# Weight sums of two outer products moved from GpSimd to VectorE, with a shorter lookahead around them

## The chip, the cores and the metric

The kernel runs on one core of one Trainium2 chip. The core has a matrix engine (TensorE, PE in the profile; its weight loads are a row of their own, PEld), VectorE (DVE), ScalarE (ACT), GpSimd (POOL) and SyncE (SP), which here issues most DMAs. Each engine works through its own queue in order, and semaphores order the engines among each other. The metric is the device time of a launch in microseconds.

## The reference

Two residual layers over x of shape (2, 2048, 512), all in fp32. Biases and selections are cut to what matters:

```python
def layer0(x):                       # wi, wo chosen by type_label (one of 3 used), swi, swo shared
    s0 = relu(x @ swi[0]) @ swo[0]   # 512 -> 2048 -> 512
    s1 = relu(x @ swi[1]) @ swo[1]
    eo = relu(x @ wi[label]) @ wo[label]
    gate_in = concat([eo[:, 0], s0[:, 0], s1[:, 0]])
    w = softmax(relu(gate_in @ g1) @ g2)
    return eo * w[0] + s0 * w[1] + s1 * w[2]

x = x + layer0(x)
x = x + (x @ W[cat] + b[cat])        # 512 -> 512, one matrix for each batch entry
```

Nearly all the work is in the three two-matrix layers of `layer0`.

## The kernel before

**Units.** The tokens are cut into four blocks of 1024. A unit is one block through one pair of matrices. There are twelve: shared pair 0 over four blocks (units 0 to 3), shared pair 1 over four, and the pairs chosen by the label over two blocks each. A unit has a first half `up` (x times the first matrix, then ReLU; "kind 0" in the code) and a second half `down` (times the second matrix; "kind 1").

**Products.** Each multiplication is a two-level block scheme that needs 7 products instead of 8 at each level: 7 outer products `i`, each with 7 inner products `k`, so 49 weight tiles (128 x 4 x 128) for each half. Products 1, 2 and 4 of a level use plain blocks of the weights; products 5, 6, 7 and 3 use sums and differences of blocks. `make_tops` (L726) and `outer_sum` (L912) make the sums on the side of the activations on VectorE; they are 128x1024 sums in `down`.

**The first unit.** Units 1 to 3 load ready sums of the weights from the scratch tensors `ws`. Unit 0 has none and makes them on the chip (class `First`, L507). `outer2` and `sum_of` make an outer sum of a whole quarter of the matrix, as four sums of 128x512 for kind 1, on GpSimd, in place of a quarter that is read no more. `take` (L598) gives one weight tile: for `k` of 1, 2 or 4 a view of the quarter in SBUF; for `k` of 5, 6, 7 or 3 it calls `make` (L621), which makes one 128x512 sum into a new buffer of the pool `w` (12 buffers). `make` also queues a store of the tile to `ws`, on SP; `flush(3)` holds the last three stores back. In `down` of unit 0 the outer products come in the order 1, 2, 3, 7, 6, 5, 4, and each needs four such sums. In the text below (2; 5) is the inner sum 5 of outer product 2.

**Order of the work.** `SLOTS_DN` (L433) is an order written out by hand: 49 slots of four matmuls each. In `down` (L894) a slot issues its matmuls (L945), then calls `used_w` (L642), then issues the eviction of its result from PSUM. The evictions on VectorE are L959 (`dz`, the seed of another accumulation), L967 (`ds`, a snapshot), L969 (`y`, block y22, which the slot of product 3 needs before it can write the same bank), L976 and L978 (`y`). After the eviction comes one step of a job, the activation sums of the next outer product (L744 to L751, L916). `y_sums` (L922) are sums of results near the end of the half.

`used_w` counts the weight tiles used, over both halves, and lets `fetch_w` (L469) go twelve tiles ahead; for unit 0 `fetch_w` calls `take`. So the place of a weight sum in the queue of its engine is set by how far `fetch_w` runs ahead. `may` (L593) holds back the first tile of outer products 3 and 7 until the last tile of products 1 and 2 is used, since their outer sums overwrite those quarters.

In `make` line 630 chooses the engine: in `up` GpSimd for outer products 4 and 3, VectorE for the others; in `down` GpSimd for all.

**Beside it.** In the same half TensorE transposes the next block of x (L309) in eight slots, ScalarE evicts what needs no sum, and at the end GpSimd begins the activation sums of the next unit (`x_sums`, L361).

Of the kernel before, what the change touches and what calls it, by code (L numbers as in the profile page):

```python
# [18 lines left out]
NP = 7  # L19
# [17 lines left out]
def cond_resid_kernel(  # L37
# [22 lines left out]
    nc = tc.nc  # L60
# [395 lines left out]
    def ready(e, kind, part, need):  # L456

        if (e, kind) not in preps:
            return e == 0
        prep = preps[e, kind]  # L460
        if prep.left[part] and need:
            while prep_bg[0] is not prep:
                for other in "ost":
                    prep_bg[0].force(other)
                prep_bg.pop(0)
            prep.force(part)
        return not prep.left[part]

    def fetch_w(upto):  # L469
        while w_next[0] < min(upto, len(w_order)):  # L470
            n, kind, i, k = w_order[w_next[0]]
            e = units[n][0]
            si, sk = SLOT_A[i], SLOT_A[k]
            part = ("t" if sk >= 4 else "s") if si >= 4 else "o" if sk >= 4 else None
            if n == 0 and not begin.may(kind, i, k, w_used[0]):
                return
            if part and not ready(e, kind, part, w_next[0] < w_used[0] + 2):
                return
            w_next[0] += 1
            if n == 0 and begin.take(kind, i, k):  # L480
                continue
            t = wp.tile([P, NG, P], F32, tag="w", name=f"w_{n}_{kind}_{i}_{k}")
            flat = t.rearrange("p g f -> p (g f)")
            if si >= 4 and sk >= 4:
                nc.sync.dma_start(out=flat, in_=ws[e, kind, "t"][:, (si - 4) * 4 + sk - 4, :])
            elif si >= 4:
                nc.sync.dma_start(out=flat, in_=ws[e, kind, "s"][:, (si - 4) * 4 + sk, :])
            elif sk >= 4:
                nc.sync.dma_start(out=flat, in_=ws[e, kind, "o"][:, PLAIN_A[si] * 4 + sk - 4, :])
            else:  # L490
                (a, c), (b, d) = divmod(si, 2), divmod(sk, 2)
                row, col = 2 * a + b, 2 * c + d
                if kind == 0 and e < 2:
                    nc.sync.dma_start(out=flat, in_=swi_v[:, e * DC + row, col, :])
                elif kind == 0:
                    src = wi_v[:, bass.ds(label[e - 2] * DC + row, 1), col, :]
                    nc.sync.dma_start(out=flat, in_=src.rearrange("p o f -> p (o f)"))
                elif e < 2:
                    nc.sync.dma_start(
                        out=t, in_=swo_v[:, e * 4 + row, :, col * P : (col + 1) * P]  # L500
                    )
                else:
                    src = wo_v[:, bass.ds(label[e - 2] * 4 + row, 1), :, col * P : (col + 1) * P]
                    nc.sync.dma_start(out=t, in_=src.rearrange("p o g f -> p (o g) f"))
            w_tiles[n, kind, i, k] = t

    class First:  # L507
# [73 lines left out]
        def outer2(self, i):  # L581
            q = lambda k: self.q[1, k]
            make = lambda *args: self.sum_of(nc.gpsimd, 1, *args)
            if i == 2:
                yield from make(5, self.space2, q(0), q(4), ADD)
                yield from make(6, q(0), q(5), q(1), SUB)
            elif i == 3:
                yield from make(3, q(1), q(2), q(6), SUB)
            elif i == 7:

                yield from make(7, q(2), q(4), q(6), SUB)
# [29 lines left out]
        def make(self, kind, i, k, blk):  # L621
            t = wp.tile([P, NG, P], F32, tag="w", name=f"w_0_{kind}_{i}_{k}")
            self.made[kind, i, k] = t
            x0, x1, op = {
                5: lambda: (blk[0], blk[4], ADD),
                6: lambda: (self.made[kind, i, 5], blk[1], SUB),
                7: lambda: (blk[1], blk[0], SUB),
                3: lambda: (blk[2], self.made[kind, i, 6], SUB),
            }[k]()
            eng = nc.gpsimd if kind == 1 or i in (4, 3) else nc.vector  # L630
            eng.tensor_tensor(t, x0, x1, op)
            self.flush(3 if kind else 1)
            si, sk = SLOT_A[i], SLOT_A[k] - 4
            if si < 4:
                o = ws[0, kind, "o"][:, PLAIN_A[si] * 4 + sk, :]
            else:
                o = ws[0, kind, "t"][:, (si - 4) * 4 + sk, :]
            self.late.append((o, t.rearrange("p g f -> p (g f)")))

    w_used = [0]  # L640

    def used_w():  # L642
        w_used[0] += 1
        fetch_w(w_used[0] + 12)

# [106 lines left out]
    def up(n, xg, tops, y):  # L754
# [12 lines left out]
        for j, i in enumerate(I_UP(n)):  # L767
# [32 lines left out]
            for s, (bk, k, d) in enumerate(SEQ_UP):  # L800
# [17 lines left out]
                if all(kk != k for _, kk, _ in SEQ_UP[s + 1 :]):  # L818
                    used_w()
# [74 lines left out]
    def down(n, H, tops, y, prepare):  # L894
# [39 lines left out]
        def slot(i, name):  # L934
# [9 lines left out]
            for g in range(NG):  # L944
# [6 lines left out]
                    skip_group_check=True,  # L951
                )
            used_w()
            if k == 1:
                z = bank[i, "z"] = ps.tile([P, TQ], F32, tag="z", name=f"dz_{n}_{i}")
# [431 lines left out]
```

## Time and profile before

| | |
|---|---|
| median of three runs | 2229.15 us (2228.36 to 2230.01) |
| the profiled execution | 2225.8 us |
| its span, first to last instruction | 2224.0 us |
| mean granted clock of TensorE | 0.997 |
| first half of unit 0 (to the first matmul of L945) | 0 to 113.55 us |
| second half of unit 0 (to the next unit's first matmul) | 113.55 to 212.10 us |

A line of the page's groups gives the source line, the engine, the operation and the shapes; a line of a timeline gives start, duration, engine, line, operation, output <- input, the count, and in brackets the idle time before it with what ended it. The durations of instructions that wait for a shared resource hold that wait. The granted clock is a share of TensorE's full clock.

### The profile page before, as it was taken

The numbers are of one execution on the slowest core, as the hardware profiler recorded it, in microseconds if no ns is written. First come the engines' busy times: TensorE is split into PE (matmuls) and PEld (weight loads), VectorE is DVE, ScalarE is ACT, GpSimd is POOL, SyncE is SP. The second block draws the span as 40 slices with busy tenths as digits, with TensorE's granted clock in tenths as the row PEclk, the third lists the DMA queues.
The fourth block names the chain that finished last, engine by engine and source line by source line (L and its number), as shares of the span: only waits on it lengthen the run. The fifth ranks groups of instructions, "written<-read, shape, count | busy, mean of one in ns | idle before, by whom it ended". The sixth has DMA issues, their size and how long they took to land.

```text
span 2224.0 us, 29253 instructions
## 1 busy us (share of the span) xinstructions
PE 2184.7 (98%) x9808; PEld 1851.8 (83%) x9808; DVE 1627.8 (73%) x2047; ACT 544.3 (24%) x937; POOL 811.9 (37%) x1259
## 2 busy tenths in 40 slices
PE   8999999999999999999999999999999999999999
PEld 6787888888888888888888888888877877887785
DVE  7897787687587587588587588588676746867695
ACT  3221231331321321231231141131133133213310
POOL 5887533852840540450450451360033023002400
PEclk9999999999999999999999999999999999999999
DMA  9853997997996996896997997896896697679681
GB/s 341 319 178 98 340 326 218 340 328 233 298 306 211 316 315 200 285 328 185 294 316 223 302 302 236 272 337 205 298 297 192 185 314 237 183 236 318 215 282 52
DMA packets 484256, 581.59 MB, mean 262 GB/s; under 512 B 28552, under 2 KB 316296, under 8 KB 480908
## 3 DMA queue, kind: packets, MB, share of 16 engines
q1 hardware_dynamic: 480380, 572.91, 79.4%
q10 hardware_dynamic: 3728, 6.82, 0.9%
q8 instruction: 80, 1.31, 0.2%
q14 instruction: 68, 0.56, 0.1%
HBM read 421.80 MB, written 157.81 MB: 261 GB/s over the span
## 4 chain that ended last, share of the span: by engine, by line
PE 85%; DVE 7%; DMA 2%; issue 1%; SPq 0%; ACT 0%; DVEq 0%; ACTq 0%
PE dx L945 23%; PE ux L810 23%; PE dy L945 11%; PE uy L810 11%; PE dz L945 6%; PE uz L810 6%; PE po L1159 5%; DVE h L916 1%; DMA w<-ws_t 1%; DVE h L787 1%; DVE t L749 1%; DMA w<-in_L_cond_W_dram 1%; DVE t L747 1%; DVE t L744 1%; DVE t L751 0%
## 5 line engine op out<-in xcount | busy, mean ns | idle before, releaser
L810 PE MATMUL ux<-xs,w 128*128 128x256 f32 x1792 | 426.2, 380 | 10.0 <-DVE uz L827 5.0
L945 PE MATMUL dx<-t,w 128*128 128x256 f32 x1680 | 397.4, 379 | 3.3 <-DVE ds L967 3.1
L810 PEld LDWEIGHTS ux<-xs,w 128*128 128x128 f32 x1792 | 338.9, 190 | 69.8 <-DVE uz L827 8.0
L945 PEld LDWEIGHTS dx<-t,w 128*128 128x128 f32 x1680 | 318.1, 190 | 48.7 <-issue 2.4
L1196 POOL TENSOR_TENSOR mix<-mix 128x512 f32<-128x512 f32 x72 | 110.1, 1531 | 443.0 <-ACT mix L1191 355.3
L833 DVE TENSOR_TENSOR us<-ux,h 128x512 f32<-128x512 f32 x240 | 163.2, 687 | 128.3 <-PE ux L810 128.0
L916 DVE TENSOR_TENSOR h<-h,h 128x1024 f32<-128x1024 f32 x192 | 246.4, 1297 | 0.0
L781 ACT ACTIVATE h<-h 128x1024 f32<-128x1024 f32 x156 | 163.9, 1054 | 235.0 <-DVE h L838 122.4
L810 PE MATMUL uy<-xs,w 128*128 128x256 f32 x896 | 212.5, 380 | 2.1 <-DVE h L857 1.9
L838 DVE TENSOR_TENSOR h<-uy,us 128x512 f32<-128x512 f32 x168 | 116.0, 691 | 119.6 <-ACT us L831 115.5
L692 POOL TENSOR_TENSOR seen<-pulse 1x1 f32<-1x1 f32 x33 | 16.9, 513 | 509.7 <-DVE pulse L691 473.2
L810 PEld LDWEIGHTS uy<-xs,w 128*128 128x128 f32 x896 | 169.7, 190 | 30.0 <-DVE h L857 4.3
L844 ACT ACTIVATE h<-uz 128x512 f32<-128x512 f32 x168 | 99.5, 592 | 351.4 <-PE uz L810 312.2
L945 PE MATMUL dy<-h,w 128*128 128x256 f32 x672 | 159.7, 381 | 4.2 <-DVE y L969 4.1
L810 PE MATMUL ux<-xi,w 128*128 128x256 f32 x640 | 152.2, 380 | 5.1 <-DVE us L833 2.9
L945 PEld LDWEIGHTS dy<-h,w 128*128 128x128 f32 x672 | 127.4, 190 | 22.8 <-issue 5.2
L945 PE MATMUL dx<-h,w 128*128 128x256 f32 x616 | 145.5, 379 | 0.0
L945 PE MATMUL dz<-h,w 128*128 128x256 f32 x616 | 145.5, 379 | 0.0
L857 DVE TENSOR_TENSOR h<-uy,us 128x512 f32<-128x512 f32 x168 | 112.1, 686 | 44.0 <-PE uy L810 42.2
L810 PEld LDWEIGHTS ux<-xi,w 128*128 128x128 f32 x640 | 120.5, 190 | 25.1 <-issue 7.2
L141 POOL TENSOR_TENSOR po<-pr 128x384 f32<-128x384 f32 x48 | 54.5, 1136 | 232.5 <-DMA pr<-in_L_cond_wo_dram 82.4
L787 DVE TENSOR_TENSOR h<-h,h 128x1024 f32<-128x1024 f32 x96 | 135.4, 1410 | 3.2 <-ACT h L844 1.9
(155 smaller groups left out, 3432.9 us busy)
## 6 DMA issues: line engine op xcount, KB each, us to landing
w<-ws_t SPq DMA_DIRECT2D x352, 256.0 KB, 4.2
w<-ws_s SPq DMA_DIRECT2D x270, 256.0 KB, 4.2
w<-ws_o SPq DMA_DIRECT2D x264, 256.0 KB, 4.6
xs<-xs SPq DMA_DIRECT2D x56, 896.0 KB, 7.4
ws_s<-ps SPq DMA_DIRECT2D x24, 1024.0 KB, 8.1
ws_t<-pt SPq DMA_DIRECT2D x24, 1024.0 KB, 9.5
ys<-y SPq DMA_DIRECT2D x11, 2048.0 KB, 7.8
ws_o<-po SPq DMA_DIRECT2D x24, 768.0 KB, 6.6
```

Of the source, the lines that this page charges most:

```text
L141: eng.tensor_tensor(o, i0, i1, op)
L781: nc.scalar.activation(v, v, AF.Relu)
L787: nc.vector.tensor_tensor(o, blk_of(O[22], cc), blk_of(O[21], cc), ADD)
L810: nc.tensor.matmul(p[:, g, :], lhsT=wt[:, 2 * d + g, :], rhs=x_ops[n, i, k], start=first and g == 0, stop=True, skip_group_check=True,)
L833: nc.vector.tensor_tensor(t, p, half(src, 12 if k == 6 else 22, d), ADD)
L838: nc.vector.tensor_tensor(half(dst, 22, d), bank["y", d], t, ADD)
L844: nc.scalar.activation(half(dst, 11, d), p, AF.Relu if i in final else AF.Copy)
L857: nc.vector.tensor_tensor(half(dst, 12, d), p, sn["b", d], ADD)
L916: nc.vector.tensor_tensor(bl(o), bl(i0), bl(i1), SUB)
L945: nc.tensor.matmul(p, lhsT=wt[:, g, :], rhs=op[g], start=first and g == 0, stop=True, skip_group_check=True,)
L1159: nc.tensor.matmul(po[t], lhsT=mixed[c], rhs=l1[blk][0][:, c, :], start=(c == 0), stop=(c == DC - 1),)
L1196: nc.gpsimd.tensor_tensor(m[:, 3, :, :], m[:, 3, :, :], m[:, j, :, :], ADD)
```

## The change

In `make` the engine for `down` becomes VectorE for outer products 2 and 6 and stays GpSimd for the other five; for `up` the new expression chooses as the old one did. The constant lookahead of twelve tiles becomes a function. With `NP` = 7 the list `(1, 4)` stands for the second and the fifth outer product of `down`, 2 and 6, whose tiles begin about at number 56 and 77 of the order. Until seven tiles past such a number the lookahead is at most six, though never cut back below the number itself; after that it grows by two for each tile used, until it is twelve again. Before tile 44 or so and after tile 91 it is twelve as before.

```diff
-            eng = nc.gpsimd if kind == 1 or i in (4, 3) else nc.vector
+            eng = nc.vector if i in ((2, 6) if kind else (1, 2, 6, 5, 7)) else nc.gpsimd
             eng.tensor_tensor(t, x0, x1, op)
             self.flush(3 if kind else 1)
...
     w_used = [0]
 
+    def ahead(used):
+        far = used + 12
+        for at in (1, 4):
+            first = (NP + at) * NP
+            if used < first + NP:
+                far = min(far, max(used + 6, first))
+            else:
+                far = min(far, first + NP + 2 * (used - first - NP) + 6)
+        return far
+
     def used_w():
         w_used[0] += 1
-        fetch_w(w_used[0] + 12)
+        fetch_w(ahead(w_used[0]))
```

## The prediction

> **What bounds the kernel now.** I read the engine shares first, then the chain that ended last, then the first unit's second half stage by stage, then the order of single instructions there.
>
> ```profile
> PE 2184.7 (98%) x9808; PEld 1851.8 (83%) x9808; DVE 1627.8 (73%) x2047; ACT 544.3 (24%) x937; POOL 811.9 (37%) x1259
> ...
> PE 85%; DVE 7%; DMA 2%; issue 1%; SPq 0%; ACT 0%; DVEq 0%; ACTq 0%
> ```
>
> TensorE is the bound over the whole, so time can move only where TensorE waits. The 7% of VectorE in the chain must be looked for by place. In busy time by stretch (columns: us, then busy us and instructions of PE, PEld, DVE, ACT, POOL; clock; DMA share; GB/s) the second half of the first unit is such a place. It runs from 113.55 us, its first matmul, to 212.10, the first of the next unit:
>
> ```profile
> 123.00:155.50 32.50, 30.66 (x156) 26.54 (x154) 32.43 (x24) 8.12 (x24) 30.29 (x16) 1.00 0.53 164
> 155.50:183.00 27.50, 24.10 (x101) 20.01 (x102) 27.43 (x20) 1.92 (x5) 27.27 (x13) 0.94 0.64 228
> 183.00:199.00 16.00, 15.11 (x70) 12.68 (x68) 15.86 (x19) 1.59 (x5) 3.68 (x5) 1.00 0.29 82
> ```
>
> VectorE is full from 123 to 199, GpSimd nearly full to 183, and TensorE has holes from 153 on. The timeline of TensorE gives the holes (start, duration, ..., idle before and its releaser):
>
> ```profile
> 156.05 2.59 PE L945 MATMUL dy<-h,w 128*128 128x256 f32 x8 [2.39 <-DVE y L969]
> 158.43 2.99 PE L945 MATMUL dz<-h,second 128*128 128x256 f32 x8
> ...
> 171.50 1.96 PE L945 MATMUL dy<-h,w 128*128 128x256 f32 x8 [1.44 <-DVE y L969]
> 173.62 1.99 PE L945 MATMUL dz<-h,second 128*128 128x256 f32 x8 [0.16 <-DVE dz L959]
> ...
> 180.33 1.97 PE L945 MATMUL dx<-t,w 128*128 128x256 f32 x8 [1.26 <-DVE ds L967]
> ```
>
> Later ones are 0.63, 0.26 and 0.71. All seven: 6.85 us. A slot of four matmuls has a step of 1.727 us (161.26 to 168.17 is four), a transpose 0.43. So 49 slots and 8 transposes need 88.1 us, and the half takes 98.55: **10.5 us** are lost, holes, slow clock and restarts together. That is the most that the change can win here.
>
> Why VectorE is late is in the timelines of VectorE and GpSimd:
>
> ```profile
> 112.64 1.22 DVE L749 TENSOR_TENSOR y<-h 128x1024 f32<-128x1024 f32 x1
> ...
> 153.29 2.28 DVE L916 TENSOR_TENSOR h<-h,h 128x1024 f32<-128x1024 f32 x1
> 155.49 0.41 DVE L969 TENSOR_TENSOR y<-dy,ds 128x256 f32<-128x256 f32 x1
> 155.82 1.95 DVE L751 TENSOR_TENSOR t<-h,t 128x1024 f32<-128x1024 f32 x1
> ```
> ```profile
> 107.89 1.27 POOL L631 TENSOR_TENSOR w<-w,second 128x512 f32<-128x512 f32 x1
> ...
> 161.06 2.25 POOL L631 TENSOR_TENSOR w<-second 128x512 f32<-128x512 f32 x1
> 163.27 2.25 POOL L631 TENSOR_TENSOR w<-second,w 128x512 f32<-128x512 f32 x1
> 165.48 2.25 POOL L631 TENSOR_TENSOR w<-second 128x512 f32<-128x512 f32 x1
> ```
>
> Alone, VectorE's 128x1024 sum takes 1.22 us (step 1.14) and GpSimd's 128x512 sum 1.27. Together each is 2.25 to 2.28, step 2.21: they take turns. So a **pair** costs 2.21, and one GpSimd sum adds 2.21 - 1.14 = 1.07 us to the VectorE sum beside it. Evictions that read PSUM (0.41, step 0.34) aren't slowed.
>
> **The change part by part.** Removed from GpSimd: eight sums, (2; 5, 6, 7, 3) and (6; 5, 6, 7, 3). Added to VectorE: the same eight. No row of before shows them there, but line 631 has sums of this size on VectorE in the first half: 676 to 705 ns alone, step 0.62 by the evictions of that size, and 1.74 to 1.76 us beside GpSimd. So 0.62 us (0.55 to 0.70) where GpSimd is idle, and 0.62 + 1.07 = 1.69 where it has a sum ready.
>
> By the Trainium skill ("GPSIMD Engine Reference", when an elementwise sum belongs on which engine) a two-input fp32 sum is 1.96 times slower on GpSimd than on VectorE, so it should go to VectorE. The row agrees in size (1.27 against 0.68) and the plain sum of shared time would be 8 x 0.62 - 8 x 1.07 = -3.6 us. I don't take it: three of the removed sums ran at 105.6 to 110.4, where only PSUM evictions were beside them, and what counts is when VectorE gets to each eviction. So I walk its queue.
>
> *Lookahead.* A sum enters VectorE's queue behind the matmuls of a slot and before that slot's eviction. With six tiles ahead, (2;5) and (2;6) come after slot 52 (counted over both halves; slot 49 starts at 113.55), (2;7) after 54, (2;3) after 57; (6;5) and (6;6) after 73, (6;7) after 75, (6;3) after 78. GpSimd's own sums move in program order only: its queue holds nothing else here, so it runs as soon as buffers allow, as before. The eight stores (256 KB, 2.0 us to land) keep their order on SP; those of product 5 now queue behind those of product 6, to about 180, while the next reader of ws comes in unit 1's second half. Unit 1's first weight load is asked for at use 89 instead of 87: two slots, 3.5 us, against over 15 us of lead and 3.0 us to land. I cost both at nothing; without that cover they would be worth up to 3.5 us.
>
> *To slot 70.* (2;5) and (2;6) run at about 120 to 121 beside no GpSimd sum (it waits for TensorE until 120.7): 1.24 us, of which VectorE's 0.88 us idle at 121.9 takes most; the rest shifts. From there VectorE has 1.24 us more, and its saving is not there: GpSimd has one sum less, (2;3), but moves its next one up, so 16 of its sums still fall before the eviction y22 of product 3 (16 between 120.7 and 155.5 before). By the walk that eviction comes at 158.0 instead of 155.49: **+2.5 us**, 4 x 0.62. TensorE's slot 70 waits for it.
>
> *To slot 77.* From y22 of product 3 to that of product 7 before: 155.49 to 170.94, with 7 GpSimd sums between. After: again 7 (the last three sums of product 5, four of product 4, one slot of buffer wait before the latter), and (6;5), (6;6) in front of the eviction, 1.24 us, and 0.36 of phase: 175.05, **+4.1 us**. Slot 77 starts at 175.5 instead of 171.50.
>
> *From slot 77 on* comes the gain. GpSimd is done at 174 instead of 183.2, so VectorE runs alone: (6;7) and (6;3) cost 0.62 each and the holes of before (0.16, 1.26, 0.63, 0.26) close. 21 slots x 1.727 = 36.3, plus the hole of 0.7 at slot 94 that comes from the next unit's sums on GpSimd and stays: end at 212.5, against 212.1. So +0.4 us before the clock.
>
> *Clock.* Behind the hole of 2.39 us the granted clock by the microsecond was:
>
> ```profile
> 156.00:157.00 1.00, 0.95 (x5) 0.88 (x6) 1.00 (x1) 0.00 (x0) 1.00 (x2) 1.00 1.14 463
> 157.00:158.00 1.00, 1.00 (x4) 0.80 (x3) 1.00 (x2) 0.00 (x0) 1.00 (x1) 0.62 1.03 418
> 158.00:159.00 1.00, 1.00 (x4) 0.80 (x3) 1.00 (x1) 0.00 (x0) 0.92 (x2) 0.50 1.05 434
> ```
>
> 0.50 and 0.67 followed: 1.7 us lost. Before, that loss is free, since slot 77 waited for VectorE anyway. After, the first hole's loss is free in the same way, but slot 77's own hole (2.9 to 4.6 us) is followed by TensorE-bound slots, so its 1.7 counts. The Trainium skill ("TensorE: Matmul & The Clock Gate", what the clock gate does) speaks of an idle window of some 3.4 us before half clock, and of phase by chance. By it the first hole goes unpunished, the second is then 4.6 and is punished: the same +1.7. By the row (2.39 us was enough, 1.44 was not) both are punished. If neither is, +0.4; a hole of 5.96 us at 22 us had half clock for 6 us, so up to 3.1. I take 1.7, by the nearest row.
>
> Sum: 212.5 + 1.7 - 212.1 = **+2.1 us**. The rest is TensorE-bound and carries it through. The profiled execution took 2225.8 us (span 2224.0 and 1.8 around it), so 2227.9; the median of the runs is 3.35 higher: **2231.3 us**, +0.1%. From no change, a measurement here tells about 0.2%, 4.5 us.
>
> **The rivals.**
> 1. *The shared time saved does show.* For: 3.6 us less in sum, and the holes from slot 77 on vanish (3.75 us with 1.44). Against: two thirds of VectorE's new work lies before GpSimd runs dry. It decides if product 2's sums fit into slack before 123 us, so that y22 of product 3 is no later than 155.5 and its hole stays short of the clock's 1.7: -3.75 - 1.7 = -5.5, **2223.7 us**.
> 2. *GpSimd stays beside the moved sums: slower.* In my walk four of eight meet no GpSimd sum. If GpSimd is held up (outer sums that wait for TensorE, w buffers freed by TensorE at slots 70 to 77) so that its sums fall beside (6;7), (6;3) and the pair at 120, four more pairs cost 4 x 1.07 = 4.3: +6.4, **2235.6 us**. It decides from three such pairs on. For: the wait for buffers is real once GpSimd leads TensorE by 12 made tiles; against: only product 4's four sums wait.
> 3. *It does not do what it says:* the sums vanish in gaps of VectorE and every hole stays, **2229.2 us**. Against: VectorE is 99.7% busy from 155.5.
>
> **How the numbers follow.** Forecast 0.54 (own range 2228.5 to 2234.0, from the clock's 0 to 3.1 and a sum's 0.55 to 0.70 us), rival 1 0.15, rival 2 0.25, rival 3 0.06. Within 0.2%: 0.54 + 0.06 = 0.60; faster 0.15; slower 0.25. Signs of both kinds hold weight, so the range reaches to about the middle of both outer cases: 2224.5 to 2236.5.
>
> **What would show it.** Line 631 with 28 sums on VectorE (20 before) and 28 on GpSimd (36). GpSimd's last weight sum at about 174 (183.2). Holes at slot 70 of about 3 us ending near 158.4 and at slot 77 of about 3 us ending near 175.5, both released by L969's eviction (L981 in the changed file, twelve lines on); no hole between 178 and 204; half clock behind slot 77. Unit 1 starts at about 214. I am wrong if y22 of product 3 comes at 155.5 or earlier, if VectorE's eight sums don't stand where I put them, or if the time moves outside the first 215 us.

## The result and the profile after

The changed kernel takes 2233.28 us (median of 22 runs, 2227.39 to 2238.45) against 2228.38 us before (22 runs, 2221.55 to 2232.55): ratio 1.0024, 95% interval 1.0016 to 1.0032, so it is **4.9 us slower** by the medians, 3.6 to 7.1 us by the interval. The forecast was +2.1 us, to 2231.3 us, in a range of 2224.5 to 2236.5. The time lies inside that range. The slowdown of 0.24% is a little beyond the 0.2% that the likeliest case allowed, and the forecast's move of 0.1% lies below the measured interval.

The second half of unit 0 took 104.51 us in the profile (112.69 to 217.20), 98.55 before: +5.96. This figure, called **the half** from here on, is what the experiments are read by. The rest of the span says nothing: span less half was between 2123.9 and 2131.7 us over the fourteen profiles of this study, with no relation to the change, and was 2125.4 before and 2128.3 after. Each half comes from one profiled execution of its kernel, so how much a half varies from one execution to the next is not known. Whole times of several runs are given below with their ratio; the other kernels have one run each.

Slots are counted over both halves: slot 49 is the first of this half, slot 97 the last. A "hole" is TensorE's idle time in front of a slot. "Half clock" means that the slots behind a hole run at a granted clock of about 0.5.

Three stretches of the half on the changed kernel (columns as in the prediction: us, then busy us and instructions of PE, PEld, DVE, ACT, POOL; clock; DMA share; GB/s):

```profile
123.00:155.50 32.50, 27.92 (x135) 23.77 (x134) 30.98 (x25) 5.93 (x18) 23.34 (x13) 0.95 0.54 162
155.50:183.00 27.50, 22.47 (x92) 18.76 (x90) 26.69 (x21) 3.28 (x9) 19.37 (x10) 0.88 0.53 192
183.00:199.00 16.00, 16.00 (x76) 14.09 (x75) 14.43 (x18) 1.52 (x4) 0.00 (x0) 1.00 0.51 158
```

GpSimd has less to do, 43 us instead of 58 in the first two stretches, and TensorE still lost time in both: 27.92 busy instead of 30.66, then 22.47 instead of 24.10, at a granted clock of 0.95 and 0.88 instead of 1.00 and 0.94. Only the last stretch is full now. The timeline of TensorE on the changed kernel:

```profile
138.45 3.55 PE L957 MATMUL dx<-t,w 128*128 128x256 f32 x8 [4.17 <-DVE ds L979]
141.84 1.89 PE L957 MATMUL dx<-h,second 128*128 128x256 f32 x8
...
159.87 1.97 PE L957 MATMUL dy<-h,w 128*128 128x256 f32 x8 [0.57 <-DVE y L981]
...
176.66 3.75 PE L957 MATMUL dy<-h,w 128*128 128x256 f32 x8 [4.46 <-DVE y L981]
180.20 3.08 PE L957 MATMUL dz<-h,second 128*128 128x256 f32 x8
183.12 1.89 PE L957 MATMUL dx<-t,w 128*128 128x256 f32 x8
```

Two large holes, at slot 60 (new) and at slot 77 (1.44 us before). Slot 70, where the forecast had one, has 0.57. From one start to the next, slot 60 took 3.39 us instead of 1.727 and slots 77 and 78 took 6.46 instead of 3.45: 1.66 and 3.01 us lost to half clock. The granted clock behind the two holes, by the microsecond:

```profile
139.00:140.00 1.00, 1.00 (x4) 0.78 (x3) 1.00 (x1) 0.00 (x0) 0.18 (x1) 0.50 0.28 82
177.00:178.00 1.00, 1.00 (x3) 0.81 (x3) 1.00 (x2) 0.00 (x0) 0.00 (x0) 0.50 0.00 0
```

Between 183 and 204 us there is no hole, as forecast.

Why slot 60 waits is in the timelines of VectorE and GpSimd on the changed kernel:

```profile
119.83 0.69 DVE L631 TENSOR_TENSOR w<-second 128x512 f32<-128x512 f32 x1
120.56 1.64 DVE L631 TENSOR_TENSOR w<-w,second 128x512 f32<-128x512 f32 x1
122.12 2.29 DVE L763 TENSOR_TENSOR t<-h,t 128x1024 f32<-128x1024 f32 x1
...
125.80 1.75 DVE L631 TENSOR_TENSOR w<-second 128x512 f32<-128x512 f32 x1
...
132.23 1.42 DVE L631 TENSOR_TENSOR w<-second,w 128x512 f32<-128x512 f32 x1
...
137.99 0.41 DVE L979 TENSOR_TENSOR ds<-dx,y 128x256 f32<-128x256 f32 x1
...
159.31 0.41 DVE L981 TENSOR_TENSOR y<-dy,ds 128x256 f32<-128x256 f32 x1
...
172.57 1.74 DVE L631 TENSOR_TENSOR w<-second 128x512 f32<-128x512 f32 x1
174.35 0.69 DVE L631 TENSOR_TENSOR w<-w,second 128x512 f32<-128x512 f32 x1
...
176.09 0.42 DVE L981 TENSOR_TENSOR y<-dy,ds 128x256 f32<-128x256 f32 x1
...
177.56 0.69 DVE L631 TENSOR_TENSOR w<-second 128x512 f32<-128x512 f32 x1
...
180.79 1.57 DVE L631 TENSOR_TENSOR w<-second,w 128x512 f32<-128x512 f32 x1
```
```profile
119.91 3.42 POOL L555 TENSOR_TENSOR second<-second,second 128x512 f32<-128x512 f32 x2 [3.46 <-PE dz L957]
125.46 1.55 POOL L555 TENSOR_TENSOR second<-second,second 128x512 f32<-128x512 f32 x1 [2.13 <-PE dx L957]
...
130.85 2.26 POOL L631 TENSOR_TENSOR w<-second 128x512 f32<-128x512 f32 x1
...
145.98 1.27 POOL L555 TENSOR_TENSOR second<-second,second 128x512 f32<-128x512 f32 x1 [6.79 <-PE dx L957]
...
180.55 1.26 POOL L631 TENSOR_TENSOR w<-second,w 128x512 f32<-128x512 f32 x1 [6.78 <-issue]
```

The lines of L631 on VectorE are the moved sums, product 2's first and then product 6's. Of product 2's four sums only the first is alone (0.69 us); the other three meet a GpSimd sum and take 1.42 to 1.75. The sums that they meet at 119.91 and 125.46 are the outer sum of product 3 (L555); the one at 130.85 is an inner sum of product 3. The snapshot `ds` of slot 58, on which slot 60 waits, runs 25.30 us after the half's start; before it was 19.82, and slot 60 followed without a wait:

```profile
133.37 0.41 DVE L967 TENSOR_TENSOR ds<-dx,y 128x256 f32<-128x256 f32 x1
```
```profile
134.30 1.89 PE L945 MATMUL dx<-t,w 128*128 128x256 f32 x8
```

Then TensorE is late, and GpSimd, whose last part of product 7's outer sum needs slot 62 done, is idle for 6.79 us. That lets VectorE catch up before slot 70.

### The profile page after: what moved, and what is told of

The parts are those of the page before. It is cut to its first block, busy times and chain, and to the rows that moved or that the text cites. A ratio compares the mean times of both kernels' runs of the same rounds, so it can differ in the third digit from the quotient of the medians.

```text
span 2232.8 us, 29247 instructions
## 1 busy us (share of the span) xinstructions
PE 2190.7 (98%) x9808; PEld 1854.8 (83%) x9808; DVE 1625.1 (73%) x2055; ACT 545.4 (24%) x937; POOL 792.3 (35%) x1251
## 4 chain that ended last, share of the span: by engine, by line
PE 83%; DVE 5%; DMA 4%; SPq 1%; issue 1%; POOL 0%; ACT 0%; DVEq 0%; ACTq 0%; POOLq 0%
PE dx L957 23%; PE ux L822 21%; PE dy L957 12%; PE uy L822 10%; PE dz L957 6%; PE uz L822 5%; PE po L1171 5%; DVE h L928 1%; DMA w<-ws_t 1%; DMA w<-ws_o 1%; DMA w<-in_L_cond_W_dram 1%; DVE h L799 1%; DMA ws_o<-po 0%; DMA w<-ws_s 0%; DMA g<-in_L_cond_g_dram 0%
## 5 line engine op out<-in xcount | busy, mean ns | idle before, releaser
L928 DVE TENSOR_TENSOR h<-h,h 128x1024 f32<-128x1024 f32 x192 | 244.1, 1286 | 0.0
L957 PE MATMUL dy<-t,w 128*128 128x256 f32 x576 | 136.1, 379 | 0.0
```

Of the source, the lines that this page charges most:

```text
L928: nc.vector.tensor_tensor(bl(o), bl(i0), bl(i1), SUB)
L957: nc.tensor.matmul(p, lhsT=wt[:, g, :], rhs=op[g], start=first and g == 0, stop=True, skip_group_check=True,)
```

## The experiments

The half and its holes over 1 us, with slot numbers; an asterisk marks a hole with half clock in the slot or two behind it:

| kernel | half, us | holes, us |
|---|---|---|
| before | 98.55 | 70: 2.39*, 77: 1.44, 81: 1.26 |
| the change | 104.51 | 60: 4.17*, 77: 4.46* |
| sums on VectorE, lookahead of twelve | 99.52 | 70: 4.62* |
| lookahead alone | 98.54 | 70: 2.38, 77: 3.13* |
| product 2 alone | 102.02 | 60: 4.18*, 77: 3.13* |
| product 6 alone | 99.23 | 70: 2.38*, 77: 3.71* |
| the change, without product 3's outer sum | 97.42 | 77: 4.45* |
| before, without product 3's outer sum | 95.50 | 77: 3.12* |
| the change, 13 spare matmuls at 60 and 77 | 100.67 | 60: 1.28, 77: 1.56 |
| the change, 28 spare matmuls at 60 and 77 | 103.38 | none |
| product 5 instead | 97.10 | 70: 2.36*, 77: 1.46, 91: 1.91 |
| product 5, product 6 early on GpSimd | 96.58 | 60: 2.58*, 91: 1.50 |
| products 2 and 5, product 6 early | 96.82 | 51: 1.58, 70: 2.36*, 91: 1.44 |
| the same, 6 spare matmuls at 70 | 95.76 | 51: 1.59, 70: 1.04, 91: 1.43 |

**1. The two edits apart.** The engines as in the change, with the old lookahead:

```diff
-        fetch_w(ahead(w_used[0]))
+        fetch_w(w_used[0] + 12)
```

> The eight sums on VectorE, lookahead of twelve as before. The figure to read is the second half of unit 0, from its first matmul to the next unit's first: 98.55 us before, 104.51 after. Theory A (the time is VectorE's queue: each sum delays the evictions behind it, and the hole falls where the sum stands): with twelve tiles ahead the sums of product 2 stand mostly before the half, in front of slot 49, and those of product 6 six slots earlier, in front of the eviction y22 of product 3. No hole at slot 60, a hole of 5 to 6 us at slot 70, little at slot 77; the half takes 98 to 100. Theory B (the shorter lookahead costs the time, the engine doesn't): 98.6, with the holes of before.

Half 99.52, inside theory A's range, with one large hole at slot 70:

```profile
160.71 3.75 PE L957 MATMUL dy<-h,w 128*128 128x256 f32 x8 [4.62 <-DVE y L981]
```

Theory A has the half and the place of the hole, but not every size: the hole is 4.62 us where 5 to 6 were expected, and slot 60 still has 0.92 where none was. Two of product 2's sums run ahead of the half, at 110.8 and 111.6. That shifts no cost out of sight: counted from the last wait in the first half (107.43 us before), the way to the end of the second takes 104.67 us before, 110.63 in the change and 105.64 here. The other way round, the lookahead with all sums on GpSimd:

```diff
-            eng = nc.vector if i in ((2, 6) if kind else (1, 2, 6, 5, 7)) else nc.gpsimd
+            eng = nc.vector if i in (() if kind else (1, 2, 6, 5, 7)) else nc.gpsimd
```

> The shorter lookahead alone, all sums of the second half on GpSimd. Theory A: GpSimd's queue holds nothing but these sums here, so their order and their times stay: half 98.6 us, holes of 2.4 at slot 70 and 1.4 at slot 77 as before. Theory B (the lookahead costs): 102 to 104.5.

98.54: the lookahead by itself costs nothing, and GpSimd's sums of the half keep their order and their times to within 0.02 us from the half's start. One hole differs from the expectation: slot 77 has 3.13 with half clock behind it, not 1.44:

```profile
170.15 3.54 PE L957 MATMUL dy<-h,w 128*128 128x256 f32 x8 [3.13 <-DVE y L981]
```

This time there was no half clock behind slot 70, so TensorE reached slot 77 sooner and waited longer for the same eviction; slot 77 starts 57.94 us into the half, 57.95 before. The loss of 1.65 us behind slot 77 takes the place of the hole of 1.26 and of smaller ones. With the sums on VectorE the lookahead decides where they stand, and its places are worse than the ones twelve tiles ahead: 104.51 against 99.52.

**2. The two products apart.** `(2,)` with `for at in (1,)`, and `(6,)` with `for at in (4,)`.

> Only product 2's four sums on VectorE, with the lookahead limit around it alone. Theory A: the hole of 4.2 us at slot 60 stays with its half clock, since these four sums make it; the hole at slot 77 is 3 to 3.5 us instead of 4.5; half 100 to 101.5 us. Theory C (only product 6's sums cost, since GpSimd has no work at first when product 2's are made): half 98.6.

102.02, half a microsecond beyond the range of theory A, with the hole of slot 60 as in the full change:

```profile
138.57 3.41 PE L957 MATMUL dx<-t,w 128*128 128x256 f32 x8 [4.18 <-DVE ds L979]
```

> Only product 6's four sums on VectorE, with the lookahead limit around it alone. Theory A: slot 60 has no hole, slot 70 the 2.4 us of before, slot 77 a hole of 4 to 5 us with half clock behind it; half 99.5 to 101.5 us. Theory C: 104.5, all of the loss.

99.23, less than theory A's least, and the hole at slot 77 is 3.71 where 4 to 5 were expected. So product 2 costs 3.5 us, product 6 only 0.7: the hole at slot 77 grows, and the ones behind it (1.26, 0.63, 0.26 before) are gone. The two together cost 6.0, more than 3.5 + 0.7. The delay at slot 77 is not what adds up to more: from the half's start, that slot begins 4.5 us late with product 2 alone, 2.3 with product 6 alone, 6.0 with both. What is left from slot 77 to the end is 1.05 and 1.58 us shorter than before with one product, and only 0.06 shorter with both: the holes behind slot 77 can be closed only once, and the half clock there takes 3.0 us with both, 1.8 and 1.5 with one.

**3. The sums that product 2's meet.** Product 3's outer sum is left out, so that this part of the result is not computed; its stores stay (the diff is shortened by the lines that queue them):

```diff
-            if kind == 1 and (i, k) in ((3, 1), (7, 1)):
+            if kind == 1 and (i, k) == (3, 1):
+                self.q[1, 3] = self.q[1, 1]          # unsummed; the four stores are queued as before
+            if kind == 1 and (i, k) == (7, 1):
```

> The changed kernel with the four GpSimd sums of product 3's outer sum left out (the quarter goes into product 3 unsummed, so that part of the result is not computed); their stores stay. GpSimd then has nothing beside VectorE's product 2 sums between 115 and 127 us. Theory A1 (the hole at slot 60 comes from GpSimd sums that take turns with VectorE's new ones there): no hole over 1 us at slot 60, half 99 to 101 us instead of 104.5, since the hole at slot 77 stays. Theory A2 (VectorE's four new sums of 0.62 us alone make it late): the hole at slot 60 stays near 3 to 4 us, half 103 to 104.5.

> The kernel before with product 3's outer sum left out in the same way (that part is not computed), as the measure for the run of the changed kernel without it (97.42 us). Theory A1 (most of the change's 6 us come from VectorE's new sums meeting these four GpSimd sums): the half takes 95.5 to 97, so that without them the change costs 0.5 to 2 us. Rival (the sums on VectorE cost the same without them): 91.5 to 93.

97.42 for the change and 95.50 for the kernel before: the change costs 1.92 us here, 5.96 in full. Two thirds of the loss hang on GpSimd's sums beside product 2's. These are more than the four that were left out: in both kernels the inner sums of product 3 no longer wait for them and run earlier. In the change they run before product 2's sums (the last is at 114.11), and GpSimd has nothing more to do until product 7's outer sum at 127.28:

```profile
114.11 1.27 POOL L637 TENSOR_TENSOR w<-second 128x512 f32<-128x512 f32 x1
127.28 1.27 POOL L555 TENSOR_TENSOR second<-second,second 128x512 f32<-128x512 f32 x1 [11.90 <-DVE w L637]
```

The half itself came out lower than expected in the first of the two, since the whole second half has four GpSimd sums less, which the expectation had not taken off; the kernel before without them gives that measure. VectorE's timeline in the change without the outer sum shows product 2's sums at the length of a sum alone, and TensorE has no hole at slot 60:

```profile
122.24 0.68 DVE L637 TENSOR_TENSOR w<-second 128x512 f32<-128x512 f32 x1
122.96 0.69 DVE L637 TENSOR_TENSOR w<-w,second 128x512 f32<-128x512 f32 x1
123.57 1.22 DVE L769 TENSOR_TENSOR t<-h,t 128x1024 f32<-128x1024 f32 x1
...
126.45 0.68 DVE L637 TENSOR_TENSOR w<-second 128x512 f32<-128x512 f32 x1
...
131.02 0.68 DVE L637 TENSOR_TENSOR w<-second,w 128x512 f32<-128x512 f32 x1
```
```profile
136.48 1.89 PE L963 MATMUL dx<-t,w 128*128 128x256 f32 x8
```

**4. The clock.** Spare matmuls, whose result nobody reads, in front of slots 60 and 77 of the changed kernel:

```diff
+            if n == 0 and (i, name) in ((2, "x7"), (7, "y3")):
+                pd = ps.tile([P, D], F32, tag="m", name=f"warm_{s}")
+                for c in range(28):
+                    nc.tensor.matmul(pd[:, :P], lhsT=ident, rhs=ones, start=True, stop=True)
             slot(i, name)
```

> The changed kernel with 28 spare matmuls of 128x128 (3.0 us) in front of slots 60 and 77, whose result nobody reads: they fill most of the two holes and keep the clock up. Clock theory (behind the two holes TensorE lost 1.66 and 3.0 us to half clock, and both count): half 99.5 to 101 us. Rival (the second loss only is real, since after slot 60 VectorE sets the pace again): 101.2 to 102. If the clock is no cause: 104.5 or more.

103.38, none of the three. The 28 matmuls took 6.25 us, not the 3.0 that the expectation gave them, and overran the two holes by about 2.0 and 1.8 us. With 13 instead:

> As the run with 28 spare matmuls in front of slots 60 and 77, with 13 in their place: 28 took 6.25 us, longer than the holes, so that they overran them by 2.0 and 1.8 us; 13 take 2.9. Clock theory (the 1.66 and 3.0 us behind the two holes both count): half 99.5 to 100.5 us, equal to 103.38 less the two overruns. Rival (only the second counts): 101.2 to 102. If the clock is no cause: 104.5.

100.67, just above the clock theory's range and outside the rival's:

```profile
132.47 3.07 PE L1042 MATMUL warm<-ones,ident 128*128 128x128 f32 x26
136.82 1.99 PE L957 MATMUL dx<-t,w 128*128 128x256 f32 x8 [1.28 <-DVE ds L979]
...
168.83 3.06 PE L1042 MATMUL warm<-ones,ident 128*128 128x128 f32 x26
173.46 1.97 PE L957 MATMUL dy<-h,w 128*128 128x256 f32 x8 [1.56 <-DVE y L981]
```

The granted clock is 1.00 behind both. So 3.84 us of the change's half hang on the clock, of the 4.67 counted behind its two holes. The first loss counts too, against the rival: slot 60 starts 25.77 us into the half, as in the change (25.76), but slot 77 starts at 62.41 instead of 63.97. This share and the one of experiment 3 overlap, since the half clock behind slot 60 belongs to both.

**5. Other places for the sums.** Product 5 instead of products 2 and 6: `(5,)` and `for at in (5,)`.

> Product 5's four sums on VectorE instead of products 2 and 6, with the lookahead limit around it. They stand behind slots 80 to 84, when GpSimd is done. By theory A the first holes stay as before, GpSimd is done at about 173, the holes at slots 81 and 83 close, and a new one of about 1.4 us comes at slot 91: half 97.3 to 98.3 us.

97.10, 1.45 us less than before and 0.2 below the range. Product 5's sums start at 178.7 to 189.1, behind GpSimd's last sum (172.8 to 175.0), and take 0.68 to 0.69 us each; the first is

```profile
178.72 0.69 DVE L631 TENSOR_TENSOR w<-second 128x512 f32<-128x512 f32 x1
```

The new hole at slot 91 is 1.91 us, without half clock. Then product 6's sums early on GpSimd, in three spare buffers and one of `w` (the diff is shortened; `blocks_of` stands for the lookup of the quarter's four blocks):

```diff
+            if kind == 1 and (i, k) == (3, 1):
+                for kk in (5, 6, 7, 3):
+                    self.make(1, 6, kk, blocks_of(self.q[1, 6]))
             if kind == 1 and (i, k) in ((3, 1), (7, 1)):
```

> As with product 5 on VectorE, and product 6's four sums stay on GpSimd but stand in its queue ahead of product 3's outer sum, where it sat idle for 5 us at 110 and more until 126; three of them go to buffers of their own. Theory A: the taking of turns between 158 and 167 goes, slot 77 has no hole, 1.4 us are left at slot 91; half 94 to 96 us, 3 to 4 us less than before in all (ratio 0.998 to 0.999). If GpSimd's sums cost VectorE as much at 110 to 115 as at 160: 97.5 to 98.5.

96.58, a miss by 0.6 us: slot 77 has 0.24 as expected, but a hole of 2.58 with half clock came at slot 60. GpSimd now ran without a gap from 107 to 123 us, and VectorE's activation sums from 113 to 124 took 2.17 to 2.33 us each, the length beside a GpSimd sum; that this made the hole was not tested by a run of its own. Over all, 2225.35 us (14 runs) against 2226.71 (19): ratio 0.9991, interval 0.9979 to 1.0002, not told from no change. Product 2 as well on VectorE, at the full lookahead, so that GpSimd has room for product 6 at 104 to 110:

> Products 2 and 5 on VectorE, product 2 at the full lookahead of twelve (its sums then stand in the first half, where they met no hole), product 5 with the limit of six; product 6's four sums on GpSimd in the time that product 2's leave at 105 to 111, ahead of product 3's outer sum. Theory A: hole at slot 60 under 1.5 us, slot 70 under 2.5, none at slot 77, 1.5 to 2 at slot 91; half 93.5 to 96 us, in all 3 to 5 us less than before (ratio 0.998 to 0.999). If VectorE's sums in the first half hold TensorE up there: the first half takes 1 to 2 us longer and the gain is gone.

96.82, above its range: slots 60 and 77 are clear, but slot 51 waits 1.58 us for ScalarE, whose copy of slot 49's result stands behind a ReLU that waited for VectorE, and slot 70 keeps its 2.36 with half clock. The first half was not held up: from its last wait to slot 49 it took 6.12 us, as before. In all 2225.75 us (14 runs) against 2226.20 (19), ratio 0.9992, interval 0.9977 to 1.0006, again not told from no change. Last, that kernel with six spare matmuls at slot 70:

> The kernel with products 2 and 5 on VectorE and product 6 early on GpSimd, with six spare matmuls (1.3 us) in front of slot 70, whose hole of 2.36 us had 1.7 us of half clock behind it and no hole at slot 77 to hide it. Clock theory: hole about 1.0 us, no half clock, half 95.0 to 95.6 us instead of 96.82, 3 us less than before (ratio about 0.9985). If the loss behind slot 70 is hidden by the hole at slot 91: 96.5 to 97.

```profile
155.46 1.50 PE L1053 MATMUL warm<-ones,ident 128*128 128x128 f32 x12
158.00 1.96 PE L968 MATMUL dy<-h,w 128*128 128x256 f32 x8 [1.04 <-DVE y L992]
159.80 1.89 PE L968 MATMUL dz<-h,second 128*128 128x256 f32 x8
```

No half clock, half 95.76, 0.2 above the range of the clock theory and below the rival's. In this profile slot 49 itself waits 0.80 us, which stands ahead of the half and is not in the figure; counted from the last earlier wait of the first half, the way to the end takes 102.84 us, 102.94 without the spare matmuls and 104.67 before. From slot 70 to the end the half is 1.09 us shorter than without the spare matmuls (50.73 against 51.82); that is the clock's part. In all 2223.04 us (22 runs) against 2226.88 (27): ratio **0.9982**, interval 0.9975 to 0.9990, faster than the kernel before and, by the two ratios, than the change. What the spare matmuls alone add to the whole time is not shown: this interval and the one without them overlap.

## Why the prediction was right and where it was wrong

The direction was right, and so was most of the mechanism. The step to slot 70 was not, nor were the sizes that rest on it and the size of the clock's term. That the time still fell inside the stated range is luck as far as the sum goes: it had +2.1 us in the half where +5.96 came, and the width of the range covered it.

*What bounds the half* held. VectorE sets TensorE's pace there, it takes turns with GpSimd, and the plain sum of shared time (-3.6 us) was the wrong guide: GpSimd's busy time fell by 15 us in the first two stretches and the half got longer.

*The plain sum* that the prediction did not take has one wrong reading beside it: of the three removed sums at 105.6 to 110.4 the first, 2.25 us long, did meet an activation sum on VectorE, and only the other two ran beside evictions alone. Nothing in the forecast rests on it.

*Lookahead.* Right in the places of the sums (line 631 has 28 on each of the two engines, as said) and in its own cost: 98.54 with it alone.

*To slot 70* is the step that failed, in place and size. It said that (2;5) and (2;6) run "at about 120 to 121 beside no GpSimd sum", and in the same line that GpSimd waits until 120.7. Two sums of 0.62 us from 120 on end after that. GpSimd's line before is

```profile
120.70 3.57 POOL L555 TENSOR_TENSOR second<-second,second 128x512 f32<-128x512 f32 x2 [3.40 <-PE dz L945]
```

and the same sums started at 119.91 in the new profile, which is 120.77 by the old half's start; (2;6) started 0.65 us later and paid 1.64, and the activation sum behind it paid 2.29. The forecast also watched only the eviction y22 of product 3. The eviction that TensorE needed first was the snapshot of slot 58: 25.30 - 19.82 = 5.5 us late, where the slack was some 0.5 (slot 60 started 0.93 us after that snapshot before, 0.46 after). So slot 60 starts 5.0 us late, 4.2 of them as its own hole and most of the rest as a wait of 0.41 at slot 57, and 1.66 of half clock follow that the sum did not have.

y22 of product 3 came 4.7 us later than before (46.62 against 41.94 from the half's start), not 2.5; since TensorE was late itself by then, slot 70's hole shrank to 0.57. The 2.5 does not follow from its own terms either: 1.24 less the idle 0.88, and 1.24 more, make 1.6. The 16 GpSimd sums in that stretch are 16 in the new profile too. By an estimate from the two timelines, the 4.7 are the four sums' own 2.5, some 0.6 of added idle time of VectorE (waits of 0.64 and 0.81 for TensorE in place of the 0.88), and by subtraction some 1.6 of more time spent taking turns.

*To slot 77.* The increment was nearly right: y22 of product 7 came 6.0 us later (63.40 against 57.39), 1.3 more than at product 3; the forecast had 1.6 more. Slot 77 starts 6.0 us later in the half, not 4.0: the error of the step before, carried on.

*From slot 77 on.* The holes of before closed, as said. GpSimd's sums but one were done at 173.8 (174 forecast); the last waited 6.78 us. The profile names no releaser, but its buffer, the one of (7;3) twelve tiles earlier, is last read by slot 77, whose matmuls end at 180.4, and the sum starts at 180.55. It met (6;3), which took 1.57 us instead of 0.69. That waiting was in the forecast, but not that it could put a sum beside (6;3).

*Clock.* The mechanism was right, the size was not: 3.0 us behind slot 77 where 1.7 was taken, near the upper bound of 3.1. It also left out slot 60's 1.66, which experiment 4 shows was not free. From slot 77 to the end took 40.54 us, 38.7 in the forecast.

*The sum*: +5.96 in the half in place of +2.1, of which about 2.0 comes from slot 77's later start, 1.3 from the clock, and the rest (0.5) from short waits and longer first steps around slots 91 and 94 that the sum left out. The medians moved by 4.9, and their interval holds 5.96.

*The rivals.* Rival 2 named part of what happened. Five of the eight sums met a GpSimd sum, (2;6) and (6;3) among them as it had them, but by its own sign, three such pairs, it does not decide: there were two, and (6;6), which the forecast had as a meeting, ran alone. Its +6.4 us lies inside the measured interval, the forecast's +2.1 does not; as a time it was 2.3 us too high, the forecast 2.0 too low. Its price, 1.07 us for a meeting, was right (0.69 against 1.75 us), but one meeting more than forecast does not reach the loss; the hole's place and its half clock made the rest. Rival 1's way is open in principle: product 5's sums, put where GpSimd is done, shorten the half by 1.45 us.

## What to carry to other kernels

When two engines take turns, moving work from the slow one to the fast one saves in the sum and can still lose, because the moved piece now stands in the fast engine's queue, in front of the results that the critical engine waits for. Go through that queue to the first result that the critical engine needs, not to the one that was late before, and to a fraction of a microsecond, for a meeting with the other engine's piece can more than double its price (0.69 to 1.75 us here). Put moved work where the other engine is idle, and count each new hole with the clock behind it.

## What the runs showed of the hardware

The same hole had three outcomes. At slot 70 a hole of 2.38 or 2.39 us was followed by half clock from the second slot on (before: 0.7 us lost in the first slot, 1.1 in the second), by half clock at once (product 6 alone), or by none (lookahead alone):

```profile
157.54 3.65 PE L957 MATMUL dy<-h,w 128*128 128x256 f32 x8 [2.38 <-DVE y L981]
161.01 1.90 PE L957 MATMUL dz<-h,second 128*128 128x256 f32 x8
```
```profile
154.70 1.97 PE L957 MATMUL dy<-h,w 128*128 128x256 f32 x8 [2.38 <-DVE y L981]
156.50 1.89 PE L957 MATMUL dz<-h,second 128*128 128x256 f32 x8
```

The first fence is the kernel with product 6 alone, the second the one with the lookahead alone. In the halves of this study six holes lie between 2.36 and 2.58 us; five were followed by a loss of 1.7 to 1.8 us and one by none. Nine holes of 3.1 to 4.6 us were each followed by a loss, of 1.5 to 3.0 us. Holes up to 1.91 us in these halves were followed by none, but that is no safe limit: in the first half of the run with the sums alone on VectorE, a wait of 1.18 us at 76.41 us, 2.3 us behind one of 0.50, was followed by a slot of 3.39 us instead of 1.80 at a granted clock of 0.50, while the same two waits before and in the change cost nothing. The Trainium skill ("TensorE: Matmul & The Clock Gate", "What's actually happening") says that the window which decides runs freely. That would make it a matter of phase, which fits outcomes that differ behind equal holes. The idle window of some 3.4 us that it names does not fit: here shorter holes were enough, and the measurement decides.

Spare matmuls in the hole (1.5 to 3.1 us in the profile) kept the granted clock up at all three places where they were tried in a fitting size, slots 60 and 77 of the change and slot 70 of the last kernel, and did not delay the awaited slot, since they ended before its result was there.
